# TensorE transposes in two halves with strided weight reads, and two weight preparations moved earlier

## The chip, the cores and the metric

The kernel runs on one NeuronCore of a Trainium2 chip. The metric is device time of one execution in microseconds (us), lower is better; the median of several runs is compared. The engines are TensorE (PE, matrix products; its weight loads are listed apart as PEld), VectorE (DVE), ScalarE (ACT), GpSimd (POOL) and SyncE (SP). SP, ACT and POOL issue DMA transfers. Each engine works through its own instructions in order and waits on semaphores for the others.

## The reference

All arrays are fp32: x is (4, 512, 512), so there are four batches b of 512 rows. The first half is a gated scan, the second a feed-forward network (FFN) with a Hadamard transform:

```python
n = layernorm(x)
i, f, g = n @ Wi.T, n @ Wf.T, n @ Wg.T
gate = sigmoid(f);  v = silu(i) * (1 - gate)
o[t] = gate[t] * o[t-1] + v[t]                  # along the 512 rows of a batch
o = o * rsqrt(mean(o*o) + eps) * gnorm_w * silu(g)
x = x + layernorm(o @ Wo.T)
h = layernorm(x)
h = fwht(silu(h @ W1.T) * (h @ W3.T))           # 2048 wide, scaled by 1/sqrt(2048)
x = x + layernorm(h @ W2.T)
```

The Hadamard transform stands between h and W2, so the kernel applies it to W2 once instead of to every h.

## The kernel before, in words

**Seven products.** Every matrix product is done with Strassen's scheme in Winograd's form: both operands are split in 2x2 blocks, sums of blocks are formed ("combined") by DVE, and seven block products P1, P2, P6, P5, P7, P3, P4 are issued in this order by `seven` (line 378). The left operand has the sums S1 to S4 (`combine_left`, lines 120 to 125), the right one T1 to T4 (`combine_right`, lines 127 to 132). P1 and P2 use plain blocks. P6 is the first that needs sums, S2 and T2. The products go to three PSUM banks X, Y and Z: P1, P6, P7 and P4 to X, P2 to Y, P5 and P3 to Z. ACT copies P1, P6, P5 and P4's new values out of the bank and DVE adds the others (lines 400 and 402), and a product that adds to a bank has to wait until the bank's values of the step before are read.

**Units.** `attn_unit(b, u)` computes the projections of one batch: u = 0 and 1 are Wi and Wf for two halves of the columns, followed by the gates and the scan; u = 2 is Wg, followed by the output gate and the normalisation's squares. `attn_out(b)` multiplies by Wo, adds to x, and normalises the result for the FFN. `ffn_unit(b, m)`, m = 0 to 7, computes W1 and W3 for a share of the 2048 columns, and `ffn_out(b, part)` multiplies two units' results by W2.

**Order on PE.** PE and SP run in exactly the order in which the program is written. A queue `fill` holds small steps of other work; `run` (line 97) takes one step from it after each of the seven products where the unit is dense, or after the second, fourth, sixth and seventh where it isn't. The order on DVE, ACT and POOL is chosen by a scheduler from priorities (`tc.high_priority`) and from `behind(what)` (line 207), which holds instructions back until the instruction recorded as `read[what]` has been placed.

**Activations on PE's right side.** `normalize_tiles` (line 236) computes mean and variance of 128 rows by DVE (lines 251, 252), the power by POOL (line 221), the bias by DVE (line 229), and applies them with one ACT instruction a tile (line 262). Three batches' inputs (`ON_TENSOR`, line 234: the scan's input of batches 0 and 1 and the FFN's of batch 0) are then transposed by PE in `transpose` (line 323): 16 transposes of 128x128 (line 334) into four PSUM banks, copies by ACT and DVE (lines 339 and 341), and the sums T1 to T4. For these the ACT instruction reads its row permuted, every fourth element first, so that the columns of each transpose lie side by side. The other batches go through DRAM and a 32x32 DVE transpose.

**Weights.** Wi, Wf, Wg, W1 and W3 are loaded with batch 0 or 1, combined by DVE (`combine_weights`), stored to DRAM in combined form by POOL (`kept`, line 138), and loaded again for the next batches (`again`, line 145). Wo is scaled by gnorm_w, combined and stored by `prepare_wo` (line 585). W2 is transformed in two steps: the high step multiplies eight pieces (`load_w2`, line 614; `transform_high`, line 624) by a 128x128 Hadamard matrix and stores them; the low step reads eight tiles back (`load_low`, line 635), multiplies them by a block-diagonal one (`transform_low`, line 653), combines and stores them. High steps fill the units of batch 0, low steps the FFN units of batch 0. Weight tiles lie in two pools, five buffers and four; a load into a buffer waits until the last reader of its old content is done, and all loads behind it in SP's queue wait with it.

Of the kernel before, what the change touches and what calls it, by code (L numbers as in the profile page):

```python
# [11 lines left out]
F32 = mybir.dt.float32  # L12
AF = mybir.ActivationFunctionType
ALU = mybir.AluOpType
P = 128
# [27 lines left out]
def kernel(  # L43
# [41 lines left out]
    def bank(name):  # L85
        return psum.tile([P, 2, H], F32, tag="ps", name=name)
# [146 lines left out]

    ON_TENSOR = ("a", 0), ("a", 1), ("f", 0)

    def normalize_tiles(b, name, i0, n):

        if (name, b) not in xns:
            xns[name, b] = work.tile(
                [P, NT, D], F32, tag="wide", name=f"xn_{name}_{b}", bufs=3
            )
        t = xns[name, b]
        st = small.tile([P, n, 6], F32, tag=f"st{n}", name=f"st_{name}_{b}_{i0}")
        mv = small.tile([P, n, 2], F32, tag=f"mv{n}", name=f"mv_{name}_{b}_{i0}")
        for k in range(n):  # L250
            nc.vector.bn_stats(st[:, k, :], xs[b][:, i0 + k, :])
            nc.vector.bn_aggr(mv[:, k, :], st[:, k, :])
        r, nb, read["nb"] = scales(mv, EPS, f"{name}_{b}_{i0}")
        for k in range(n):
            x_t, to = xs[b][:, i0 + k, :], t[:, i0 + k, :]
            if (name, b) in ON_TENSOR:
                x_t = x_t.rearrange("p (k c) -> p c k", c=ND)
                to = to.rearrange("p (c k) -> p c k", c=ND)
            else:
                x_t = x_t.rearrange("p (i a c) -> p i c a", c=ND, a=32)  # L260
                to = to.rearrange("p (i c a) -> p i c a", c=ND, a=32)
            nc.scalar.activation(  # L262
                to, x_t, AF.Identity, bias=nb[:, k : k + 1], scale=r[:, k : k + 1]
            )
        if (name, b) not in ON_TENSOR:
            if (name, b) not in xnd:
                xnd[name, b] = scratch.tile(
                    [NT, P, D], F32, tag=f"xn_{name}_{b}", name=f"xnd_{name}_{b}"
                )
            nc.gpsimd.dma_start(  # L270
                out=xnd[name, b][i0 : i0 + n].rearrange("t p d -> p t d"),
                in_=t[:, i0 : i0 + n, :],
            )

    def normalize(b, name, n=2):
        for i in range(0, NT, n):
            normalize_tiles(b, name, i, n)
# [42 lines left out]

    xts = {}

    def transpose(b, name):

        xn = xns.pop((name, b))
        xt = work.tile([P, 7, 2, H], F32, tag="xt", name=f"xt_{name}_{b}", bufs=2)
        pt = [bank(f"pt_{name}_{b}_{c}") for c in range(ND)]  # L330
        for h in range(2):
            for i in range(2 * h, 2 * h + 2):
                for c in range(ND):
                    nc.tensor.transpose(pt[c][:, h, ts(i % 2, P)], xn[:, i, ts(c, P)], ident)
        with tc.high_priority(offset=URGENT):
            for c in range(ND):
                to = xt[:, B11 : B12 + 1 : B12 - B11] if c < 2 else xt[:, B21 : B22 + 1]
                if c % 2:
                    nc.scalar.copy(to[:, :, c % 2, :], pt[c])
                else:  # L340
                    nc.vector.tensor_copy(to[:, :, c % 2, :], pt[c])  # L341
            combine_right(xt, nc.vector)
        xts[name, b] = xt

    folds = {}

# [29 lines left out]
    def seven(name, multiply, quarter, done=None, add=False, by_tile=False):  # L376

        ps = {}

        def make(what, a, bb, which, first):
            if first:
                ps[which] = bank(f"{which}_{name}")
            multiply(ps[which], a, bb, first)
            split = by_tile and what == "P4"  # L390
            q = {"P1": (0, 0), "P5": (1, 1), "P6": (0, 1), "P2": (0, 0), "P7": (1, 1),
                 "P3": (0, 1), "P4": (1, 0)}[what]
            to = quarter(*q)
            with tc.high_priority(offset=URGENT):
                if split:
                    for t in range(2):
                        nc.vector.tensor_add(to[:, t], ps[which][:, t], to[:, t])
                        done(*q, t)
                elif what in ("P2", "P7", "P3") or add:
                    read[what] = nc.vector.tensor_add(to, ps[which], to)  # L400
                else:
                    nc.scalar.copy(to, ps[which])  # L402
# [36 lines left out]
    def attn_unit(b, u, dense=False):  # L439
        def gates(d):  # L440

            v, gate = d[:, 0], d[:, 1]
            nc.scalar.activation(gate, gate, AF.Tanh, scale=0.5)
            nc.scalar.activation(v, v, AF.Silu)
            nc.vector.scalar_tensor_tensor(v, gate, 1.0, v, ALU.subtract, ALU.mult)
            nc.scalar.activation(gate, gate, AF.Identity, bias=half_t, scale=0.5)
            if u == 0:
                os_[b] = work.tile([P, 2, 2, T], F32, tag="o", name=f"o_{b}")
            for h in range(2):
                nc.vector.tensor_tensor_scan(  # L450
                    os_[b][:, u, h, :], gate[:, h, :], v[:, h, :], 0.0, ALU.mult, ALU.add
                )

        def output_gate(d):
            o = os_[b]
            og = work.tile([P, 7, 2, H], F32, tag="og", name=f"og_{b}")
            nc.scalar.activation(d, d, AF.Silu)
            for m in range(2):
                into_left(og, o[:, m], d[:, m], m)
            combine_left(og, nc.vector)  # L460
            ogs[b] = og
            nc.scalar.activation(o, o, AF.Square)
            nc.vector.tensor_add(o[:, 0], o[:, 0], o[:, 1])
            nc.vector.tensor_add(o[:, 0, 0], o[:, 0, 0], o[:, 0, 1])
# [117 lines left out]
        )  # L582


    def prepare_wo():
        w = [stream_tile(("wo", c), 0, stream2) for c in range(2)]
        for c in range(2):
            for k, blocks in enumerate(((B11, B12), (B21, B22))):
                row = (2 * k + c) * P
                nc.sync.dma_start(  # L590
                    out=w[c][:, blocks[0] : blocks[1] + 1 : blocks[1] - blocks[0]],
                    in_=wo[row : row + P].rearrange("p (n f) -> p n f", n=2),
                )
            for k, blocks in enumerate(((B11, B12), (B21, B22))):
# [5 lines left out]
        wo_t[0] = w  # L600

    NR = FF // P
    NJ = NR // 2
# [60 lines left out]

    load_w2(range(0, 1))
    load_x(0)
    load_w2(range(1, 2))
    load_attn_w(0, 0)
    load_w2(range(2, 4))
    load_attn_w(0, 1)  # L670
    load_w2(range(4, 6))
    load_x(1)
# [1 line left out]
    load_attn_w(0, 2)  # L674
    with tc.high_priority():
        normalize(0, "a", 1)
    with behind("power"):
        for make in high(0, 2):
            make()
    transpose(0, "a")  # L680
    with behind("nb"):
        combine_weights(2)
    with behind("power"):
        load_constants()
    fill.extend(high(2, NJ))
    attn_unit(0, 0)
    with behind("P2"):
        combine_weights(2)
    attn_unit(0, 1, True)
    with behind("P2"):  # L690
        normalize(1, "a")
    with behind("P3"):
        combine_weights(2)
    load_attn_w(1, 0)
    attn_unit(0, 2)
    with behind("P3"):
        prepare_wo()
    transpose(1, "a")
    while len(fill) > 1:
        slot()  # L700
    fill.extend([None] * 3 + attn_out(0))
    attn_unit(1, 0, True)
    load_attn_w(1, 1)
    attn_unit(1, 1, True)
    load_attn_w(1, 2)
    load_ffn_w(0, 0)
    load_low(0)
    load_low(1)
    attn_unit(1, 2)
    transpose(0, "f")  # L710
    combine_weights()
    for b in range(B):
        last = b == B - 1
        for m in range(NU):
            if m + 1 < NU:
                load_ffn_w(b, m + 1)
            if b == 0 and m % NS == 0:
                for k in range(m, m + NS):
                    fill.extend(transform_low(k))
            if m == 0 and not last:  # L720
                fill.extend([None] * 4 * (b > 0) + attn_out(b + 1))
# [12 lines left out]
            if m == NU - 1 and not last:  # L734
                transpose_fold(*((b + 2, "a") if b + 2 < B else (b + 1, "f")))
            ffn_unit(b, m, b == 0)
            combine_weights()
        tail = ffn_out(b, NU // NS - 1)
        if b + 2 < B:
            load_attn_w(b + 2, 0)  # L740
# [52 lines left out]
```

## Time and profile before

| | |
|---|---|
| median of 3 runs | 849.2 us (847.85 to 849.77) |
| profiled execution | 848.68 us |
| its span, first to last instruction | 846.9 us |
| PE busy | 817.6 us, 97% |
| DVE, ACT, POOL busy | 459.0, 274.3, 69.4 us |
| DMA | 169.54 MB, mean 200 GB/s |
| granted PE clock | 0.996 |

The program takes its first 46 us with the DMA engines almost fully busy, its last 10 us without PE, and PE is nearly always busy in between. Times in the text are microseconds from the start of the span, where nothing else is said. "X waits for Y" means that the engine stood idle before X until Y ended, as the profiler's semaphore events show. A matmul of fp32 values appears as two records, a transpose as one.

### The profile page before, as it was taken

To read this page: it belongs to the slowest core of one execution; us is meant where nothing else is said; L and a number is where in the kernel's file an instruction comes from. 1 tells how busy PE (TensorE), PEld (TensorE's weight loads), DVE (VectorE), ACT (ScalarE), POOL (GpSimd) and SP (SyncE) were. 2 spreads that over 40 slices of the span, in tenths; PEclk is the share of its full clock that TensorE was granted. 3 is DMA by queue.
4 is the path that set the end of the run, shared out by engine and by line. 5 is a ranking of instruction groups with operands and counts; after the bars stand their busy time and mean duration, and the time that the engine had idled before them with its cause. 6 is when DMAs were issued, how large, how long until landed. Compare 5 with 4: busy or idle time off the path is not lost.

```text
span 846.9 us, 9792 instructions
## 1 busy us (share of the span) xinstructions
PE 817.6 (97%) x3728; PEld 701.1 (83%) x3728; DVE 459.0 (54%) x914; ACT 274.3 (32%) x376; POOL 69.4 (8%) x112
## 2 busy tenths in 40 slices
PE   5999989999999999999999999999999999999995
PEld 3778868878878888888888888888888888888884
DVE  5458667674747556548245544836335434633445
ACT  4563364352412224425421122424322121222111
POOL 4110010120201001002100000101100000100000
PEclk9999999999999999999999999999999999999998
DMA  9976376668889823925563822754343742625101
GB/s 331 399 260 274 113 238 235 243 257 318 300 290 346 245 87 110 405 106 199 170 231 116 266 87 87 283 202 175 136 179 94 299 158 103 224 87 217 62 26 50
DMA packets 65743, 169.54 MB, mean 200 GB/s; under 512 B 4768, under 2 KB 40224, under 8 KB 65696
## 3 DMA queue, kind: packets, MB, share of 16 engines
q1 hardware_dynamic: 56528, 125.65, 42.5%
q0 software_dynamic: 8448, 41.96, 12.4%
q10 hardware_dynamic: 720, 1.31, 0.4%
q8 instruction: 29, 0.48, 0.2%
q14 instruction: 18, 0.15, 0.0%
HBM read 125.90 MB, written 42.99 MB: 199 GB/s over the span
## 4 chain that ended last, share of the span: by engine, by line
PE 81%; DVE 6%; DMA 4%; ACT 4%; issue 2%; POOL 1%; SPq 0%; POOLq 0%; ACTq 0%; DVEq 0%
PE X_f L415 23%; PE X_po L548 11%; PE Z_f L415 11%; PE X_a L415 8%; PE Z_po L548 6%; PE Y_f L415 5%; PE Z_a L415 4%; PE X_y L501 3%; PE Y_po L548 3%; PE Y_a L415 2%; PE Z_y L501 2%; ACT xn_a L262 1%; DMA wi<-s_wi 1%; DMA x<-in_x_dram 1%; PE Y_y L501 1%
## 5 line engine op out<-in xcount | busy, mean ns | idle before, releaser
L415 PE MATMUL X_f<-xt_f,w 128*128 128x256 f32 x1024 | 242.2, 380 | 2.0 <-ACT d_f L402 1.1
L415 PEld LDWEIGHTS X_f<-xt_f,w 128*128 128x128 f32 x1024 | 193.7, 190 | 33.9 <-ACT d_f L402 3.3
L402 ACT COPY d_f<-X_f 128x512 f32<-128x512 f32 x96 | 56.1, 584 | 302.6 <-PE X_f L415 278.3
L415 PE MATMUL Z_f<-xt_f,w 128*128 128x256 f32 x512 | 121.2, 379 | 0.4 <-ACT d_f L402 0.4
L548 PE MATMUL X_po<-w,ht 128*128 128x256 f32 x512 | 120.9, 379 | 0.2 <-DVE f L400 0.2
L415 PEld LDWEIGHTS Z_f<-xt_f,w 128*128 128x128 f32 x512 | 97.1, 190 | 16.0 <-ACT d_f L402 1.2
L548 PEld LDWEIGHTS X_po<-w,ht 128*128 128x128 f32 x512 | 97.2, 190 | 13.7 <-DVE f L400 0.6
L400 DVE TENSOR_TENSOR f<-X_po,f 128x512 f32<-128x512 f32 x51 | 35.1, 689 | 90.4 <-PE X_po L548 90.1
L430 DVE TENSOR_TENSOR ht<-d_f 128x1024 f32<-128x1024 f32 x32 | 39.0, 1219 | 66.7 <-ACT d_f L524 53.0
L548 PE MATMUL Z_po<-w,ht 128*128 128x256 f32 x256 | 60.6, 379 | 1.8 <-DVE f L400 1.8
L415 PE MATMUL Y_f<-xt_f,w 128*128 128x256 f32 x256 | 60.5, 379 | 0.0
L548 PEld LDWEIGHTS Z_po<-w,ht 128*128 128x128 f32 x256 | 48.6, 190 | 8.7 <-DVE f L400 2.2
L415 PEld LDWEIGHTS Y_f<-xt_f,w 128*128 128x128 f32 x256 | 48.6, 190 | 8.3 <-issue 1.2
L221 POOL TENSOR_TENSOR rs_f<-rs_f,power 128x2 f32<-128x2 f32 x16 | 15.8, 990 | 442.4 <-DVE nm_f L304 419.6
L402 ACT COPY d_a<-X_a 128x512 f32<-128x512 f32 x36 | 21.1, 586 | 90.8 <-PE X_a L415 74.6
L400 DVE TENSOR_TENSOR d_f<-X_f,d_f 128x512 f32<-128x512 f32 x32 | 22.1, 690 | 27.0 <-PE X_f L415 27.0
L400 DVE TENSOR_TENSOR d_f<-Z_f,d_f 128x512 f32<-128x512 f32 x32 | 22.1, 689 | 26.4 <-PE Z_f L415 26.4
L415 PE MATMUL X_a<-xt_a,wi 128*128 128x256 f32 x128 | 33.1, 381 | 1.3 <-DVE xt_a L341 1.3
L524 ACT ACTIVATE d_f<-d_f 128x1024 f32<-128x1024 f32 x32 | 33.8, 1055 | 0.9
L415 PE MATMUL X_a<-xt_a,wg 128*128 128x256 f32 x128 | 30.4, 381 | 2.5 <-ACT d_a L402 1.6
L415 PE MATMUL X_a<-xt_a,wf 128*128 128x256 f32 x128 | 32.8, 379 | 0.0
L415 PEld LDWEIGHTS X_a<-xt_a,wi 128*128 128x128 f32 x128 | 24.1, 190 | 8.1 <-issue 3.3
(154 smaller groups left out, 998.8 us busy)
## 6 DMA issues: line engine op xcount, KB each, us to landing
w<-s_w SPq DMA_DIRECT2D x80, 896.0 KB, 6.3
s_w<-w POOLq DMA_DIRECT2D x24, 896.0 KB, 5.0
w<-in_W_dram SPq DMA_DIRECT2D x32, 256.0 KB, 5.9
wi<-s_wi SPq DMA_DIRECT2D x6, 896.0 KB, 10.3
wf<-s_wf SPq DMA_DIRECT2D x6, 896.0 KB, 7.4
wg<-s_wg SPq DMA_DIRECT2D x6, 896.0 KB, 5.2
wo<-s_wo SPq DMA_DIRECT2D x6, 896.0 KB, 9.4
w_h<-w2p POOLq DMA_DIRECT2D x8, 512.0 KB, 7.2
```

Source lines behind the costliest of these rows:

```text
L221: read["power"] = nc.gpsimd.tensor_tensor(r, r, power_t[:, 0:n], ALU.pow)
L262: nc.scalar.activation(to, x_t, AF.Identity, bias=nb[:, k : k + 1], scale=r[:, k : k + 1])
L400: read[what] = nc.vector.tensor_add(to, ps[which], to)
L402: nc.scalar.copy(to, ps[which])
L415: nc.tensor.matmul(ps[:, n, :], w[:, a, c, :], xt[:, bb, c, :], start=first and n == 0 and c == 0, stop=c == 1, skip_group_check=True,)
L430: nc.vector.tensor_mul(to.rearrange("p (t k) f -> p k t f", t=2), a.rearrange("p k (t f) -> p k t f", t=2), b2.rearrange("p k (t f) -> p k ...
L501: nc.tensor.matmul(ps[:, t, :], og[:, a, c, ts(t, P)], w[c][:, bb, :], start=first and t == 0 and c == 0, stop=c == 1, skip_group_check=True,)
L524: nc.scalar.activation(d[:, 0], d[:, 0], AF.Silu)
L548: nc.tensor.matmul(ps[:, t, :], hts[b, m][:, a, ts(t, P)], w[m][:, bb, :], start=first and t == 0 and m == ms[0], stop=m == ms[-1], skip_g ...
```

## The change

1. The ACT instruction of the three batches on PE reads and writes its rows in order. Instead the transpose reads its operand, which PE loads as weights, with a step of four elements (`xn[:, i, c::ND]`).
2. `transpose` becomes `transposes`, which returns two steps, one for each half of the rows. Each step does eight transposes and its own copies; the right sums follow the second. The steps are put into `fill`, so that they run between the products of the unit before (for batch 0: the first half in front, the second after the first product).
3. In batch 0 the third piece of w2 is loaded ahead of wi and wf; ACT's copies for the second and third piece are held behind the normalisation; unit 0 is dense and unit 1 isn't.
4. Batch 1's normalisation moves from unit 1 to unit 2, its statistics behind P3 of unit 1 and its ACT instructions behind a copy in unit 2.
5. Wo is loaded ahead of batch 1's wi and wf, and prepared behind P2 of unit 2.
6. The low steps 0 and 1 of w2 run in batch 1's units 1 and 2, and those of the FFN units run two tiles further on. Their loads move with them in SP's queue.
7. The Silu of the output gate is done in two halves, and weights are combined behind P7 of the unit before.

```diff
-        for k in range(n):
-            x_t, to = xs[b][:, i0 + k, :], t[:, i0 + k, :]
-            if (name, b) in ON_TENSOR:
-                x_t = x_t.rearrange("p (k c) -> p c k", c=ND)
-                to = to.rearrange("p (c k) -> p c k", c=ND)
-            else:
...
+        def apply():
+            for k in range(n):
+                x_t, to = xs[b][:, i0 + k, :], t[:, i0 + k, :]
+                if (name, b) not in ON_TENSOR:
...
+                read["xn"] = nc.scalar.activation(
+                    to, x_t, AF.Identity, bias=nb[:, k : k + 1], scale=r[:, k : k + 1]
...
+        if later:
+            return apply
+        apply()
...
-    def transpose(b, name):
+    def transposes(b, name):
...
+        def make(h):
+            if h == 0:
+                pt.extend(bank(f"pt_{name}_{b}_{c}") for c in range(ND))
             for i in range(2 * h, 2 * h + 2):
                 for c in range(ND):
-                    nc.tensor.transpose(pt[c][:, h, ts(i % 2, P)], xn[:, i, ts(c, P)], ident)
...
+                    nc.tensor.transpose(pt[c][:, h, ts(i % 2, P)], xn[:, i, c::ND], ident)
+            with tc.high_priority(offset=URGENT):
+                for c in range(ND):
+                    to = xt[:, (B11, B12)[h] if c < 2 else (B21, B22)[h], c % 2, :]
+                    if c % 2:
+                        nc.scalar.copy(to, pt[c][:, h, :])
+                    else:
+                        read["xt"] = nc.vector.tensor_copy(to, pt[c][:, h, :])
+                if h:
+                    combine_right(xt, nc.vector)
+        return [partial(make, h) for h in range(2)]
...
-            nc.scalar.activation(d, d, AF.Silu)
             for m in range(2):
+                nc.scalar.activation(d[:, m], d[:, m], AF.Silu)
                 into_left(og, o[:, m], d[:, m], m)
...
-    load_w2(range(1, 2))
+    load_w2(range(1, 3))
     load_attn_w(0, 0)
-    load_w2(range(2, 4))
+    load_w2(range(3, 4))
...
+    first, second = transposes(0, "a")
     with behind("power"):
-        for make in high(0, 2):
+        for make in high(0, 1):
             make()
-    transpose(0, "a")
-    with behind("nb"):
+        with behind("xn"):
+            for make in high(1, 2) + [first] + high(2, 3):
+                make()
+    with behind("xt"):
         combine_weights(2)
...
-    fill.extend(high(2, NJ))
-    attn_unit(0, 0)
+    fill.extend([second] + high(3, NJ))
+    attn_unit(0, 0, True)
     with behind("P2"):
         combine_weights(2)
-    attn_unit(0, 1, True)
-    with behind("P2"):
-        normalize(1, "a")
+    attn_unit(0, 1)
     with behind("P3"):
-        combine_weights(2)
+        with tc.high_priority(offset=URGENT):
+            combine_weights(2)
+        with tc.high_priority(offset=SOON):
+            apply = [normalize_tiles(1, "a", i, 2, True) for i in (0, 2)]
+    wo_t[0] = load_wo()
     load_attn_w(1, 0)
...
+    fill.extend([wo_behind_sum, norm_behind_copy] + transposes(1, "a"))
     attn_unit(0, 2)
-    with behind("P3"):
-        prepare_wo()
-    transpose(1, "a")
-    while len(fill) > 1:
-        slot()
+    load_attn_w(1, 1)
     fill.extend([None] * 3 + attn_out(0))
     attn_unit(1, 0, True)
-    load_attn_w(1, 1)
-    attn_unit(1, 1, True)
-    load_attn_w(1, 2)
-    load_ffn_w(0, 0)
     load_low(0)
     load_low(1)
+    load_attn_w(1, 2)
+    fill.extend(transform_low(0) + transform_low(1))
+    attn_unit(1, 1, True)
+    load_ffn_w(0, 0)
+    fill.extend(transposes(0, "f"))
     attn_unit(1, 2)
-    transpose(0, "f")
-    combine_weights()
+    with behind("P7"):
+        combine_weights()
...
-                for k in range(m, m + NS):
+                for k in range(m + 2, min(m + 2 + NS, NU)):
                     fill.extend(transform_low(k))
...
             ffn_unit(b, m, b == 0)
-            combine_weights()
+            with behind("P7"):
+                combine_weights()
```

`prepare_wo` is split into `load_wo`, which issues the four loads and returns the tiles, and `prepare_wo(w)`, which does the rest; `wo_behind_sum` calls it behind P2, and `norm_behind_copy` calls the two held `apply` steps behind an ACT copy.

More of the change, by code (lines that the diff above doesn't have):

```diff
@@ L234, with normalize_tiles @@
     ON_TENSOR = ("a", 0), ("a", 1), ("f", 0)
-    def normalize_tiles(b, name, i0, n):
+    def normalize_tiles(b, name, i0, n, later=False):
         if (name, b) not in xns:
@@ L253, in normalize_tiles @@
         r, nb, read["nb"] = scales(mv, EPS, f"{name}_{b}_{i0}")
-        for k in range(n):
-            x_t, to = xs[b][:, i0 + k, :], t[:, i0 + k, :]
-            if (name, b) in ON_TENSOR:
-                x_t = x_t.rearrange("p (k c) -> p c k", c=ND)
-                to = to.rearrange("p (c k) -> p c k", c=ND)
-            else:
[L260 to L268, printed above, removed]
-                )
[L270 to L273, printed above, removed]
+        def apply():
+            for k in range(n):
+                x_t, to = xs[b][:, i0 + k, :], t[:, i0 + k, :]
+                if (name, b) not in ON_TENSOR:
+                    x_t = x_t.rearrange("p (i a c) -> p i c a", c=ND, a=32)
+                    to = to.rearrange("p (i c a) -> p i c a", c=ND, a=32)
+                read["xn"] = nc.scalar.activation(
+                    to, x_t, AF.Identity, bias=nb[:, k : k + 1], scale=r[:, k : k + 1]
+                )
+            if (name, b) not in ON_TENSOR:
+                if (name, b) not in xnd:
+                    xnd[name, b] = scratch.tile(
+                        [NT, P, D], F32, tag=f"xn_{name}_{b}", name=f"xnd_{name}_{b}"
+                    )
+                nc.gpsimd.dma_start(
+                    out=xnd[name, b][i0 : i0 + n].rearrange("t p d -> p t d"),
+                    in_=t[:, i0 : i0 + n, :],
+                )
+        if later:
+            return apply
+        apply()
     def normalize(b, name, n=2):
@@ L321 @@
     xts = {}
-    def transpose(b, name):
+    def transposes(b, name):
         xn = xns.pop((name, b))
         xt = work.tile([P, 7, 2, H], F32, tag="xt", name=f"xt_{name}_{b}", bufs=2)
-        pt = [bank(f"pt_{name}_{b}_{c}") for c in range(ND)]
-        for h in range(2):
+        xts[name, b] = xt
+        pt = []
+        def make(h):
+            if h == 0:
+                pt.extend(bank(f"pt_{name}_{b}_{c}") for c in range(ND))
             for i in range(2 * h, 2 * h + 2):
                 for c in range(ND):
[L334 to L343, printed above, removed]
+                    nc.tensor.transpose(pt[c][:, h, ts(i % 2, P)], xn[:, i, c::ND], ident)
[9 more added lines that the diff above has]
+        return [partial(make, h) for h in range(2)]
     folds = {}
@@ L401, in make @@
                 else:
-                    nc.scalar.copy(to, ps[which])
+                    read["copy"] = nc.scalar.copy(to, ps[which])
             if what in ("P2", "P7", "P3", "P4") and done is not None and not split:
@@ L582, in ffn_out, with load_wo @@
         )
-    def prepare_wo():
+    def load_wo():
         w = [stream_tile(("wo", c), 0, stream2) for c in range(2)]
@@ L593, in prepare_wo @@
                 )
+        return w
+    def prepare_wo(w):
+        for c in range(2):
             for k, blocks in enumerate(((B11, B12), (B21, B22))):
@@ L599, in prepare_wo @@
             kept(("wo", c), w[c])
-        wo_t[0] = w
     NR = FF // P
@@ L684, with wo_behind_sum, norm_behind_copy @@
         load_constants()
-    fill.extend(high(2, NJ))
-    attn_unit(0, 0)
+    fill.extend([second] + high(3, NJ))
+    attn_unit(0, 0, True)
     with behind("P2"):
         combine_weights(2)
-    attn_unit(0, 1, True)
-    with behind("P2"):
-        normalize(1, "a")
+    attn_unit(0, 1)
     with behind("P3"):
-        combine_weights(2)
-    load_attn_w(1, 0)
-    attn_unit(0, 2)
-    with behind("P3"):
-        prepare_wo()
-    transpose(1, "a")
-    while len(fill) > 1:
-        slot()
+        with tc.high_priority(offset=URGENT):
[3 more added lines that the diff above has]
+    wo_t[0] = load_wo()
+    load_attn_w(1, 0)
+    while fill:
+        slot()
+    def wo_behind_sum():
+        with behind("P2"):
+            prepare_wo(wo_t[0])
+    def norm_behind_copy():
+        with behind("copy"):
+            for make in apply:
+                make()
+    fill.extend([wo_behind_sum, norm_behind_copy] + transposes(1, "a"))
+    attn_unit(0, 2)
+    load_attn_w(1, 1)
     fill.extend([None] * 3 + attn_out(0))
     attn_unit(1, 0, True)
-    load_attn_w(1, 1)
-    attn_unit(1, 1, True)
-    load_attn_w(1, 2)
-    load_ffn_w(0, 0)
     load_low(0)
     load_low(1)
+    load_attn_w(1, 2)
[3 more added lines that the diff above has]
+    fill.extend(transposes(0, "f"))
     attn_unit(1, 2)
-    transpose(0, "f")
-    combine_weights()
+    with behind("P7"):
+        combine_weights()
     for b in range(B):
```

## The prediction

> **What bounds it now.** I read the table of engines first, then the chain that ended last, then what TensorE (PE) waited for, then the windows and the timeline of the first 125 us.
>
> ```profile
> PE 817.6 (97%) x3728; PEld 701.1 (83%) x3728; DVE 459.0 (54%) x914; ACT 274.3 (32%) x376; POOL 69.4 (8%) x112
> PE 81%; DVE 6%; DMA 4%; ACT 4%; issue 2%; POOL 1%; SPq 0%; POOLq 0%; ACTq 0%; DVEq 0%
> ```
>
> PE is busy for 817.6 of 846.9 us. The change keeps all of PE's matmuls, so it can win only from the 29.3 us in which PE stands idle, and lose by new idle time or by making a PE instruction longer. The windows (columns: stretch, its length, then busy us of PE first) say where the idle time is:
>
> ```profile
> 0.00:18.05 18.05, 8.38 (x24) 3.80 (x24) 7.72 (x29) 9.08 (x11) 7.56 (x19) 1.00 0.89 314
> 18.05:46.00 27.95, 27.95 (x113) 21.58 (x114) 14.78 (x30) 12.08 (x18) 5.84 (x11) 1.00 1.02 394
> 46.00:68.90 22.90, 20.89 (x96) 16.55 (x94) 13.60 (x29) 15.59 (x20) 3.95 (x7) 1.00 0.76 284
> 68.90:110.00 41.10, 40.96 (x192) 35.69 (x192) 29.17 (x61) 17.49 (x26) 3.16 (x5) 1.00 0.44 165
> 110.00:125.00 15.00, 11.41 (x57) 9.39 (x58) 10.91 (x23) 9.48 (x10) 2.64 (x3) 1.00 0.68 238
> 410.00:830.00 420.00, 419.56 (x1945) 368.57 (x1945) 197.60 (x351) 103.58 (x149) 13.35 (x19) 1.00 0.44 156
> ```
>
> Idle: 9.7 us before 18.05, 2.0 to 68.9, 3.6 in 110 to 125, 3.5 to 410, 10.0 after 830. The last 10 us are an epilogue that the change leaves alone. The list of PE's waits names the rest:
>
> ```profile
> PE h L624 <- DMA w2p<-in_W_dram: 5.7, 1, 5.7
> PE pt_a L334 <- ACT xn_a L262: 3.5, 4, 1.9
> PE Z_a L415 <- ACT d_a L402: 1.9, 2, 1.2
> PE Z_po L548 <- DVE f L400: 1.8, 1, 1.8
> PE X_a L415 <- ACT d_a L402: 1.6, 1, 1.6
> ```
>
> The first 5.7 us are the first load. The transposes of batch 0 then wait 3.5 us for ScalarE's (ACT's) normalisation. Its duration and that of the same form without a permuted read, then the transposes' weight loads and matmuls (min/median/max ns):
>
> ```profile
> L262 ACT ACTIVATE xn_a<-x,nb_a,rs_a 128x512 f32<-128x512 f32 x16 | 20.4, 1320 | 5.2 <-DVE nb_a L229 5.2
> L307 ACT ACTIVATE y<-y,nm_y 128x512 f32<-128x512 f32 x16 | 10.6, 712 | 3.9 <-DVE nm_y L304 3.9
> L334 PEld LDWEIGHTS pt_a<-ident,xn_a x32: 138/140/143, 13.3 to 67.7; 128*128 128x128 f32 x32
> L334 PE MATMUL pt_a<-ident,xn_a x32: 272/273/329, 13.3 to 67.8; 128*128 128x128 f32 x32
> 66.21 1.91 PE L334 MATMUL pt_a<-ident,xn_a 128*128 128x128 f32 x16
> ```
>
> Sixteen transposes in 1.9 us: 0.117 us each.
>
> [...]
>
> **The parts, and their cost.** A product below is 1.73 us of PE (eight records 0.216 apart), a 128x512 transform of w2 is 0.86, a 128x256 VectorE (DVE) pass advances its queue by 0.34, a 128x512 one by 0.6, a 128x1024 one by 1.2.
>
> *The stride.* 48 transposes, three batches of 16, now load weights from every fourth column. Nothing in the trace shows this. Below: 0, if the load stays under its matmul. Nearest row: ACT's read rate halves, [...] and the pace 0.22, +0.10 us each, 4.9 us for 48. [...] I take 0.22: eight transposes then take 1.76 us, not 0.93.
>
> *Start of batch 0.* Before, ACT copied four transform results, the last at 11.48 to 12.07, before its first normalisation at 11.96. Now two come first; the second ended at 10.07, and the bias was ready at 9.95. At 0.72 a tile, overlapping, the first two tiles are ready at 11.45 and all at 12.7 (16.88 before). PE finishes the second w2 piece at 11.45, and then runs: eight transposes to 13.2, two transforms of the third piece to 14.9, first product to 16.7, eight transposes to 18.4, second product to 20.1, one transform to 21.0. Before, the third product (P6) began at 22.47 with two fewer transforms done. Gain 22.47 - 21.0 + 1.72 = 3.2. The third piece is loaded ahead of wi and wf on SP's queue: 0.5 MB at about 0.4 MB/us makes wf land near 13.4, not 12.1, hidden behind 14.9. DVE's chain (two copies, eight combinations, two copies, two xt sums) has S2 and T2 near 20.6, just before P6. The fifth w2 piece, needed near 25.3, landed at 27.1 before; with stores starting later I put it near 25 and charge 0, with 1.8 as the other end.
>
> *Unit 1 and 2 of batch 0.* The normalisation of batch 1 leaves unit 1: its 1.23 us wait (PE at 47.99 for an ACT copy behind a 1.29 us normalisation) goes. Fewer fillers add 0.25, where P6 waits for a copy behind ACT's tanh, table load and silu. Gain 1.0. Unit 2 before ran 53.27 to the next unit's P6 at 72.60: 19.33, less one transform, 18.47, with the 0.83 wait at 68.95 in it. After: six products to 10.35, transposes to 12.1, the last product at 12.55 (DVE's add of P7 sits behind combinations of wg, statistics, two scans and seven wo passes, some 15 us in one queue), to 14.3; the second half waits for DVE's copies of the first, which stand behind three wo passes and an add, to 16.5; two products to 19.95. P6 needs T2, behind two copies, two output-gate multiplies and T1: 21.1. Queued behind it are all other PE products. Loss 2.7. The split Silu lets the first multiply start 1 us sooner; it is in this sum. wo, now ahead of batch 1's wi and wf on SP, takes the slot of stored w2 pieces and is wanted 8 us after it can land; wi and wf are wanted 14 us after their slots are free.
>
> *Batch 1 to the FFN.* From P5's end in unit 1 (99.39) to the FFN's first product (124.78) were 25.39 us, with waits of 1.63, 0.69, 0.90 and 0.65. ACT's order is the cause: four normalisations of 1.32 between copies. Now they take 0.72, and four moved transforms (3.45 us) give cover. I find one wait left, 0.45. New length 25.39 - 3.87 + 0.45 + 3.45, and 1.66 for the stride: gain 3.42 - 1.66 = 1.8 after taking off work that is only moved. The FFN's first two products need the first half alone; T2 is done 4 us before its P6. Pulling low tiles 2 and 3 forward makes SP wait for the wo slots (last product of batch 0's output, about 101) ahead of the FFN's first weights, which still land 8 us before use. Their eight DVE sums and POOL stores run where DVE is busy 0.7 and POOL 0.08.
>
> *FFN of batch 0.* The 1.78 us wait at 240.51 is DVE behind a weight load; that load stood on SP behind w2 tiles waiting for a store at 222 to 231. Those tiles are now fetched two units earlier, and the combinations come behind P7: 1.5 gained. Were the store the limit elsewhere, 1.8 would come back. Combining behind P7 leaves 11 us to the next P6 for 2.7 us of DVE.
>
> *At nothing.* The copies out of PSUM become twice as many of half the size: 2 x 0.34 against 0.6 of DVE's queue each, 0.5 us for six, inside the chains above. Later batches are transposed by DMA and DVE as before; from 410 on no instruction changes, and PE idles 0.4 us there.
>
> Sum: 3.2 + 1.0 - 2.7 + 1.8 + 1.5 = 4.8. The profiled execution took 848.68 (span 846.9 and 1.8 around it); the median is 0.5 above it. Forecast 849.2 - 4.8 = 844.4.
>
> **Rivals.** *Stride free.* For it: the transposes' weight load is 140 ns, the others' 190, so it may have room under its matmul. Then 4.9 less about 1.7 that DVE and DMA waits take: +3.2, time 841.2.
> *Strided loads decide against it.* Place: the 48 transposes on PE. Without stride the gain is 8.0; some 85% of added time lies on the path, so 48 x 0.85 x e = 8.0 at e = 0.20, a pace of 0.31. [...] Against it: ACT pays only a factor of two.
> *New waits take the start's gain.* The DMA engines are 0.89 to 1.02 busy until 46; if the fifth piece lands at 27.1 or wg late, and DVE's queue in unit 2 runs 2 us longer than my sum, the 3.2 to 3.8 won go: 848.
>
> **Chances.** Forecast 0.42, free stride 0.25, waits 0.15, dear stride 0.18. Under 0.2% (1.7 us) no difference can be told in this kernel. Faster: 0.42 + 0.25 + 0.07 = 0.74; same 0.08, half of the waits case; slower 0.18. The forecast's own range, with its DMA and DVE ends, is 841 to 848. The full range, 838.5 to 851, reaches past the free stride (with no DVE waits left) and leaves out most of the dear stride, 0.14, and 0.05 below.
>
> **What would show it.** The strided weight load near 245 ns and 16 transposes spread over some 3.5 us; the third product at 21 us; no normalisation wait of PE over 1 us; waits for DVE before the last product of unit 2 and the third of the next; no wait of 1.6 us near 111, none of 1.8 near 240. It is wrong if a transpose's pace passes 0.31, or if PE waits for a w2 piece before 40 us for over 3 us.

## The result and the profile after

The changed kernel takes 840.97 us (median of 4 runs, 840.72 to 841.86), the kernel before 849.45 (4 runs, 847.85 to 849.77). The ratio is 0.9906, 95% interval 0.9889 to 0.9923. The forecast was 844.4 with 838.5 to 851 around it. The profiled execution took 841.11 us with a span of 839.3, which is 7.57 us less than the execution before. The forecast gain was 4.8, and it comes near only because its errors have both signs.

The page of the changed kernel: engines, then the chain that ended last.

```profile
PE 817.5 (97%) x3728; PEld 703.8 (84%) x3728; DVE 457.6 (55%) x920; ACT 269.1 (32%) x386; POOL 68.9 (8%) x112
...
PE 84%; DVE 5%; DMA 5%; ACT 2%; issue 2%; SPq 1%; POOL 1%; POOLq 0%; DVEq 0%; ACTq 0%
```

PE is busy for as long as before (817.5 and 817.6 us), so the gain is idle time. DMA and SP's queue, 4% and 0% of the chain before, are 5% and 1% now. The windows (stretch, length, then busy us of PE first) and the list of PE's waits (total, times, longest):

```profile
0.00:18.05 18.05, 13.04 (x45) 7.84 (x46) 9.68 (x33) 9.08 (x16) 8.07 (x20) 1.00 0.94 325
...
46.00:68.90 22.90, 22.06 (x107) 18.76 (x106) 22.02 (x49) 15.45 (x22) 5.37 (x7) 1.00 1.02 399
...
110.00:125.00 15.00, 15.00 (x73) 12.51 (x72) 14.63 (x28) 8.23 (x14) 1.06 (x2) 1.00 0.60 213
```

```profile
PE h L638 <- DMA w2p<-in_W_dram: 5.2, 2, 5.0
PE Z_f L426 <- ACT d_f L413: 4.7, 2, 4.5
...
PE X_a L426 <- DVE xt_a L130: 0.8, 1, 0.8
```

Up to 125 us, PE has lost all its waits but three: the first load, 0.18 us for a w2 piece at 35.45 and 0.84 us for T2 at 66.25. But there is a wait that the forecast doesn't have: 4.5 us for a copy by ACT, in unit 4 of batch 0's FFN. By stages, from the starts of the same products in both timelines (work that is only moved taken out):

| stage | forecast gain | measured | how |
|---|---|---|---|
| start to batch 0's third product | 3.2 | 5.4 | 22.47 to 18.74, and two transforms more done; 0.7 of it is the first load, 5.70 to 5.01 |
| units 1 and 2, to the next third product | -1.7 | 0.9 | 72.60 to 66.25, less the 5.4 above |
| batch 1 to the FFN's first product | 1.8 | 4.35 | 124.78 to 117.53, less the time won so far, and 3.45 of transforms done |
| FFN of batch 0 | 1.5 | -3.3 | 409.81 to 402.40 at a later wait that both have, less all the above |
| rest | 0 | 0.2 | |
| sum | 4.8 | 7.6 | |

So two readings had to be tested: that the strided read costs PE next to nothing, and that the FFN's new wait is made by x of batch 2 coming late, and by which part of the change.

The transposes and the normalisation up to 70 us, by tile (min/median/max ns):

```profile
L343 PEld LDWEIGHTS pt_a<-ident,xn_a x32: 195/209/221, 10.3 to 61.6; 128*128 128x128 f32 x32
```

```profile
L262 ACT ACTIVATE xn_a<-x,nb_a,rs_a x8: 799/802/815, 9.4 to 57.3; 128x512 f32<-128x512 f32 x8
```

The weight load went from 140 to 209 ns, but eight transposes started at 57.96 and the product behind them at 58.91: 0.119 us each from start to start, where the forecast has 0.117 for contiguous columns. ACT's tile went from 1320 to 802 ns.

The chain that ended last, in the changed kernel near the new wait (start, us, what):

```profile
195.91 12.70 DMA x<-in_x_dram
...
208.63 0.69 DVE st_a L252
...
213.18 1.28 ACT xn_a L262
214.46 0.48 ACT d_f L413
...
214.98 3.78 PE Z_f L426 x8
```

x of batch 2 takes 12.7 us from issue to landing. DVE's statistics wait for it, POOL's power and ACT's normalisation follow, and the copy that PE needs is queued behind the second normalised tile. Which transfers stand beside x's? First the timeline of the kernel before, then that of the changed one (start, us, queue, line, what):

```profile
199.96 0.53 POOL L138 DMA_DIRECT2D s_w<-w  x1 [1.63 <-DVE w L125]
...
204.18 2.11 SPq L116 DMA_DIRECT2D x<-in_x_dram  x4
```

```profile
195.44 2.22 SPq L116 DMA_DIRECT2D x<-in_x_dram  x4
...
196.03 0.53 POOL L138 DMA_DIRECT2D s_w<-w  x1 [19.21 <-DVE w L125]
```

The two stores of combined weights, 896 KB each, were issued at 197.80 and 199.96 before, 6.4 and 4.2 us ahead of x. Combining behind P7 put them at 196.03 and 197.03, 0.6 and 1.6 us behind x's first issue. The DMA engines, 0.05 busy from 188 to 194 us, are 1.00 and 1.04 busy in 198 to 204 and 204 to 210. (Both kernels also issue two 896 KB reloads of down weights just ahead of x.) x's median landing went from 8.0 to 12.6 us. An estimate: two stores are 1.8 MB, which take 4.6 us at the 400 GB/s of 204 to 210 us, as much as x lost.

The wait costs more than its length. The windows around it (the third number from the end is PE's granted clock):

```profile
210.00:215.00 5.00, 0.53 (x4) 0.12 (x2) 2.61 (x13) 3.02 (x4) 2.43 (x4) 0.84 0.84 251
215.00:217.50 2.50, 2.50 (x6) 2.05 (x7) 0.65 (x1) 2.50 (x3) 0.48 (x1) 0.50 0.95 388
217.50:220.00 2.50, 2.50 (x7) 1.96 (x7) 2.17 (x6) 0.30 (x1) 1.25 (x2) 0.50 0.90 372
```

After the idle stretch of 4.47 us PE runs at half clock (0.50) for 5 us, from 215 to 220, and at 0.95 from 220 to 222. The product that waited takes 3.58 to the next one's start and that one 2.54, in place of 1.73 each: 4.47 + 1.85 + 0.81 = 7.1 us.

### The profile page after: what moved, and what is told of

Its sections match the earlier page's. It is cut to its first block, busy times and chain, and to the rows that moved or that the text cites. A ratio compares the mean times of both kernels' runs of the same rounds, so it can differ in the third digit from the quotient of the medians.

```text
span 839.3 us, 9824 instructions
## 1 busy us (share of the span) xinstructions
PE 817.5 (97%) x3728; PEld 703.8 (84%) x3728; DVE 457.6 (55%) x920; ACT 269.1 (32%) x386; POOL 68.9 (8%) x112
## 3 DMA queue, kind: packets, MB, share of 16 engines
q0 software_dynamic: 8448, 41.96, 12.7%
## 4 chain that ended last, share of the span: by engine, by line
PE 84%; DVE 5%; DMA 5%; ACT 2%; issue 2%; SPq 1%; POOL 1%; POOLq 0%; DVEq 0%; ACTq 0%
PE X_f L426 23%; PE X_po L559 12%; PE Z_f L426 12%; PE X_a L426 8%; PE Z_po L559 6%; PE Y_f L426 6%; PE Z_a L426 5%; PE Y_po L559 3%; PE X_y L512 3%; DMA w2p<-in_W_dram 3%; PE Y_a L426 2%; PE Z_y L512 2%; DMA x<-in_x_dram 2%; DVE x L316 1%; PE Y_y L512 1%
## 5 line engine op out<-in xcount | busy, mean ns | idle before, releaser
L426 PE MATMUL Z_f<-xt_f,w 128*128 128x256 f32 x512 | 122.9, 384 | 4.7 <-ACT d_f L413 4.7
L221 POOL TENSOR_TENSOR rs_f<-rs_f,power 128x2 f32<-128x2 f32 x16 | 14.0, 878 | 428.7 <-DVE nm_f L308 406.8
L411 DVE TENSOR_TENSOR f<-Z_po,f 128x512 f32<-128x512 f32 x28 | 19.2, 684 | 24.9 <-PE Z_po L559 24.9
```

The source lines that it names most:

```text
L221: read["power"] = nc.gpsimd.tensor_tensor(r, r, power_t[:, 0:n], ALU.pow)
L426: nc.tensor.matmul(ps[:, n, :], w[:, a, c, :], xt[:, bb, c, :], start=first and n == 0 and c == 0, stop=c == 1, skip_group_check=True,)
```

## The experiments

The kernel before was timed again beside each group of runs. Its median was 849.67 to 849.84 us there and 849.45 beside the changed kernel, so the differences from the changed kernel below are uncertain by some 0.4 us on top of the ranges given.

### The strided weight load by itself

The kernel before, with six groups of 16 transposes put ahead of batch 1's own, differing only in the step of the columns. Their results are overwritten.

```diff
+        flat = xn.rearrange("p n d -> p (n d)")
+        if (name, b) == ("a", 1):
+            for k in range(16):
+                nc.tensor.transpose(pt[k % 4][:, k // 8, ts(k // 4 % 2, P)], flat[:, 0 : 128 : 1], ident)
+            for k in range(16):
+                nc.tensor.transpose(pt[k % 4][:, k // 8, ts(k // 4 % 2, P)], flat[:, 0 : 255 : 2], ident)
...
```

> The kernel before, with 96 more transposes put ahead of the real ones of batch 1 (six groups of 16, whose weights are 128 columns at every 1st, 2nd, 3rd, 4th, 8th and 16th fp32). Their results are overwritten, so the output is the same and the time is longer by some 12 us or more. Theory A (the slower weight load stays under the matmul before it): the weight load is near 140 ns at step 1 and 210 at step 4, [...]and rises no further at 8 and 16; steps 2 and 3 lie between; 16 transposes take 1.9 us at every step. Theory B [...]: 16 take 1.9 us at step 1 and 3.5 at step 4. A third way: the load rises again at 8 and 16 by what the bytes span[...].

It took 859.05 us in one run, beside 849.84 for the kernel before: 9.2 more, where 12 or more were expected. The tile's weight loads (lines 334, 336 and 340 are the steps 1, 2 and 4; 338, 342 and 344, left out, are 3, 8 and 16 with medians of 196, 192 and 196 ns), then PE's timeline:

```profile
L334 PEld LDWEIGHTS pt_a<-ident,xn_a x16: 139/141/142, 67.4 to 69.1; 128*128 128x128 f32 x16
L336 PEld LDWEIGHTS pt_a<-ident,xn_a x16: 194/209/209, 69.2 to 71.0; 128*128 128x128 f32 x16
...
L340 PEld LDWEIGHTS pt_a<-ident,xn_a x16: 206/211/213, 73.0 to 74.8; 128*128 128x128 f32 x16
```

```profile
67.61 1.91 PE L334 MATMUL pt_a<-ident,xn_a 128*128 128x128 f32 x16
69.35 2.08 PE L336 MATMUL pt_a<-ident,xn_a 128*128 128x128 f32 x16
...
73.08 2.10 PE L340 MATMUL pt_a<-ident,xn_a 128*128 128x128 f32 x16
75.02 1.94 PE L342 MATMUL pt_a<-ident,xn_a 128*128 128x128 f32 x16
```

Theory A holds for the pace and B falls: from one group's start to the next it is 1.74 us at step 1 and 1.94 at step 4, 0.0125 us more for a transpose, 0.6 us for 48. What theory A says of the steps between falls: step 2 loads as slowly as step 4 (209 and 211), and steps 3, 8 and 16 a little faster. Of the six steps only the contiguous one stands apart. And sixteen loads of 0.211 are 3.4 us, but lie within 2.0: the loads overlap each other, so their duration isn't their pace.

### The stride undone, and the stride alone

The first takes the strided read out of the changed kernel, the second puts only it into the kernel before.

```diff
-                if (name, b) not in ON_TENSOR:
+                if (name, b) in ON_TENSOR:
+                    x_t = x_t.rearrange("p (k c) -> p c k", c=ND)
+                    to = to.rearrange("p (c k) -> p c k", c=ND)
+                else:
...
-                    nc.tensor.transpose(pt[c][:, h, ts(i % 2, P)], xn[:, i, c::ND], ident)
+                    nc.tensor.transpose(pt[c][:, h, ts(i % 2, P)], xn[:, i, ts(c, P)], ident)
```

> The changed kernel with only the stride undone: ScalarE reads every fourth column again and the transposes read contiguous ones; order and halves stay as changed. Theory A (strided weight loads cost nothing on TensorE, ScalarE's shorter normalisation is the gain): a normalised tile takes 1.32 instead of 0.72 us, so TensorE waits for tiles 1 to 3 of batch 0 near 12 to 17 us; 2 to 4 us slower than the changed kernel, 843 to 845. Theory B (0.10 us for each of 48 strided transposes): it gains 4.9 us on TensorE and loses the same 2 to 4; 0 to 3 us faster than the changed kernel. If the wait near 215 us depends on ScalarE's timing early on, it could shift by a microsecond either way.

843.64 us (843.04 to 844.31), 2.7 slower than the changed kernel, as theory A has it. PE waits 1.07 at 15.60 and 0.88 at 109.80 for ACT, which it doesn't with the stride. The 4.48 us wait in the FFN stays.

```diff
-            if (name, b) in ON_TENSOR:
-                x_t = x_t.rearrange("p (k c) -> p c k", c=ND)
-                to = to.rearrange("p (c k) -> p c k", c=ND)
-            else:
+            if (name, b) not in ON_TENSOR:
...
-                    nc.tensor.transpose(pt[c][:, h, ts(i % 2, P)], xn[:, i, ts(c, P)], ident)
+                    nc.tensor.transpose(pt[c][:, h, ts(i % 2, P)], xn[:, i, c::ND], ident)
```

> The kernel before with only the stride: the transposes read every fourth column, ScalarE's normalisation of the transposed batches reads and writes without permutation. Theory A (the strided weight load is hidden, the normalisation takes 0.72 instead of 1.32): the waits for ScalarE at 13 to 17 us shrink from 3.5 to about 1.5, that at 48 us and those at 111 to 121 us by 1 to 3 together; 844 to 847. Theory B (0.10 us for each of 48 transposes on TensorE's path): 4.9 us of this are lost again, 848 to 852.

844.84 us (844.2 to 845.31) beside 849.74: ratio 0.9945, interval 0.9929 to 0.9961, in theory A's range. This small part alone gives 4.9 us, as much as the forecast charged for its strided reads; in the new order, by the run above, the same edit is worth 2.7. On PE's timeline the transposes now wait once:

```profile
12.36 2.86 PE L331 MATMUL pt_a<-ident,xn_a 128*128 128x128 f32 x16 [1.39 <-ACT xn_a L259]
```

The transposes' 3.5 us of waits are 1.39, all 16 go in one row, and the product behind them waits 0.42; the 1.63 at 111 us is 0.63, and the 0.69 for ACT near 118 is gone; the FFN's 1.7 us wait for DVE is as before.

### The start in its old order

The changed kernel with four transforms ahead of all 16 transposes, and the third w2 piece behind wi and wf.

```diff
-    load_w2(range(1, 3))
+    load_w2(range(1, 2))
     load_attn_w(0, 0)
-    load_w2(range(3, 4))
+    load_w2(range(2, 4))
...
-        for make in high(0, 1):
+        for make in high(0, 2):
             make()
-        with behind("xn"):
-            for make in high(1, 2) + [first] + high(2, 3):
-                make()
+    first()
+    second()
...
-    fill.extend([second] + high(3, NJ))
+    fill.extend(high(2, NJ))
```

> The changed kernel with the start of batch 0 in the old order: four transforms of w2 before the 16 transposes, these in one go, the third w2 piece behind wi and wf again. The strided read and the short normalisation stay. Theory A (the start gained 4.8 us by both, and the stride alone is 1.9 of it by the run with the permuted read): TensorE idles 2 to 4 us more before 20 us, the rest is as in the changed kernel, 843 to 845. Rival (the short normalisation alone is enough, since the tiles then come at 0.72 us each): less than 1 us slower, under 842.

843.57 us (842.39 to 844.3), 2.6 slower than the changed kernel. On PE's timeline the transposes wait 1.39 us at 12.05 for ACT's normalisation, and 0.25 and 0.21 behind that: 1.85 us of new idle time, a little under the 2 to 4 of theory A. The profiled spans differ by 1.3 only, so the size is uncertain. That the order adds to the short normalisation is clear: all four runs lie above the rival's 842.

### x one unit earlier

```diff
+            if m == 2 and b == 0:
+                load_x(2)
...
-            if m == 3 and b == 0:
-                load_x(2)
```

> The changed kernel, and the load of x of batch 2 is issued one FFN unit earlier (in unit 2 instead of unit 3 of batch 0), ahead of the w2 tiles and the down weights of that unit; its third buffer is free by then. Theory A (TensorE's 4.47 us wait at 215 us comes from x, which is issued at 195.4 and lands after 12.7 us, because VectorE and ScalarE do the statistics and the normalisation in order ahead of the unit's copies): the wait goes, with the slow clock behind it; 5 to 7 us faster than the changed kernel, 834 to 836. Rival (the DMA engines are full there, and whatever is moved only changes what is late): the down weights or w2 tiles come late instead, gain below 2 us, with a new wait for a DMA between 180 and 245 us.

834.36 us (834.05 to 834.73), ratio to the kernel before 0.9818, interval 0.9797 to 0.9839. This is 6.6 below the changed kernel, whose own ratio is 0.9906, and the fastest of all. From the list of PE's waits, the one in question:

```profile
PE Z_f L426 <- ACT d_f L413: 0.2, 1, 0.2
```

The 4.47 is gone, no other wait took its place, and the span is 7.0 shorter (832.3), against the 7.1 worked out above. Theory A holds: x's lateness was the whole of it. In 211 to 222 us PE was busy 7.02 of 11 us at clock 0.69 before this edit, and 11.00 of 11 at 1.00 with it.

### Which part makes x late

Two candidates: the order behind P7, which moved the stores, and w2's lower tiles, fetched two units earlier. The first is tried alone in the kernel before, the second undone in the changed one.

```diff
             ffn_unit(b, m, b == 0)
-            combine_weights()
+            with behind("P7"):
+                combine_weights()
```

> The kernel before with one edit: in the FFN loop the combinations of the next weights come behind the adds of P7. Theory A (this order takes a late weight load out of VectorE's way, and on the other side brings the stores beside the load of x): the 1.78 us wait at 240.5 goes; x of batch 2 lands later than its 8 us; if it is late enough, a wait for ScalarE's copy of 1 to 5 us comes near 219, so the time is between 847 and 853. Rival (the wait at 215 us of the changed kernel comes from the w2 tiles that are fetched two units earlier, not from this order): no wait over 1 us near 219, and the time is some 1.5 us below the kernel before.

855.14 us (853.72 to 855.54), ratio 1.0064, interval 1.0047 to 1.0082: slower than the kernel before, and 2 us past the range of theory A. PE waits 5.66 us at 225.10 for ACT's copy; in the timeline x and a store beside it, then DVE's statistics, stand ahead in that chain:

```profile
204.37 2.17 SPq L116 DMA_DIRECT2D x<-in_x_dram  x4
204.96 0.53 POOL L138 DMA_DIRECT2D s_w<-w  x1 [19.21 <-DVE w L125]
...
216.49 0.69 DVE L251 BATCH_NORM_STATS2 st_a<-x 128x6 f32<-128x512 f32 x1 [3.75 <-DMA x<-in_x_dram]
...
225.10 3.65 PE L415 MATMUL Z_f<-xt_f,w 128*128 128x256 f32 x8 [5.66 <-ACT d_f L402]
```

This one edit makes the wait, with no tile fetched earlier. x's median landing is 13.8 us. SP issues the down weights and x within 0.2 us of where it did in the kernel before (203.52 and 204.37, 203.32 and 204.18 before); of the transfers ahead of x and just behind it only the stores have moved, from 197.80 and 199.96 to 204.96 and 205.97. So it is the stores that make x late. The 1.78 us at 240.5 is gone, as the theory says.

```diff
+    attn_unit(1, 1, True)
+    load_attn_w(1, 2)
+    load_ffn_w(0, 0)
     load_low(0)
     load_low(1)
-    load_attn_w(1, 2)
-    fill.extend(transform_low(0) + transform_low(1))
-    attn_unit(1, 1, True)
-    load_ffn_w(0, 0)
...
-                for k in range(m + 2, min(m + 2 + NS, NU)):
+                for k in range(m, m + NS):
```

> The changed kernel without the lower transforms of w2 pulled forward: tiles 0 and 1 are loaded and transformed in the FFN again, and each pair in the unit where it was. Theory A (the four moved transforms cover ScalarE's copies at the end of batch 1): one or two waits of 0.5 to 1.6 us come back between 95 and 125 us, and a wait for VectorE behind a late weight load of 1 to 2 us near 235; the 4.47 us wait stays if the order behind P7 makes it, and goes if the early tiles do. With the wait staying 843 to 845; with it gone 836 to 838.

844.32 us (843.66 to 847.05), with this in PE's timeline:

```profile
216.25 3.78 PE L426 MATMUL Z_f<-xt_f,w 128*128 128x256 f32 x8 [5.88 <-ACT d_f L413]
```

The wait stays and is longer (x's median landing is 14.0), so the early tiles don't make it. The moved transforms cover one wait, 0.92 for DVE at 115.54; the wait of 1 to 2 us expected near 235 didn't come, so it is the order behind P7 that keeps it away, not the early tiles. A DMA wait of 1.63 at 37.6, where the changed kernel has 0.18, lies ahead of everything edited.

### Is the order behind P7 worth anything?

The changed kernel without it, with x late and with x early. Both drop the same line in the FFN loop:

```diff
-            with behind("P7"):
-                combine_weights()
+            combine_weights()
```

> The changed kernel without the order that puts the combination of the next FFN weights behind the adds of P7; the combinations' stores to memory come earlier again. Theory A1 (x of batch 2 lands late because stores of unit 4's weights were moved next to its load): the 4.47 us wait shrinks to below 1.5 us and the time is 4 to 6 us below the changed kernel, 835 to 837. Theory A2 (x is late because of the w2 tiles and down weights in front of it): x still takes over 11 us to land, the wait stays above 3 us, the time is within 1.5 us of the changed kernel.

843.87 us (843.64 to 844.38), 2.9 slower than the changed kernel. As A1 has it, the stores are early again (191.05 and 193.17), x lands after 7.8 us and the wait for ACT is 0.95. But A1's time is wrong: a new wait appears in the timeline.

```profile
231.68 0.42 DVE L122 TENSOR_TENSOR w<-w 128x256 f32<-128x256 f32 x1 [9.08 <-DMA w<-in_W_dram]
...
234.10 3.78 PE L559 MATMUL X_po<-w,ht 128*128 128x256 f32 x8 [5.04 <-DVE f L411]
```

DVE stands 9.08 us at a combination whose weights haven't landed, and the adds that PE needs are behind it. By the chain that ended last these weights were issued at 217.87 and landed after 13.1 us, and POOL issued four stores of 896 KB from 217.82 on: again stores beside a load that an in-order queue waits for. In the kernel before, DVE waits in the same way for 5.67 us up to 238.30, and PE loses its 1.78 at 240.51 by it; there the weights were issued late, at 231.69, and landed within 6.0.

> The changed kernel with both edits: x of batch 2 loaded one unit earlier, and no order behind P7. Theory A (the order behind P7 is worth the 5.04 us wait for VectorE behind a late weight load near 234, which the run without it showed, and has nothing to do with x once x is early): no wait near 214, a wait of 3 to 5 us near 232, 838 to 842. Rival (that wait was itself a follow-up of x's load between the weights): it goes too, 834 to 835.

836.65 us (836.29 to 838.0), below theory A's 838 and above the rival's 835. From its timeline:

```profile
228.95 1.99 PE L559 MATMUL X_po<-w,ht 128*128 128x256 f32 x8 [1.07 <-DVE f L411]
```

Neither alone: most of the 5.04 was a follow-up of x's load, and 1.07 is left. With x late, POOL stood 2.21 us at the store of batch 2's normalised rows, just ahead of the four stores of 217.82. With x early it has issued two by 211 and three from 215.37 on, and the weights, issued at 216.68 and 217.26, are combined at 226.52. With x early, the order behind P7 is worth 2.3 us.

### The control: x early in the kernel before

The same move of `load_x(2)` as above, in the kernel before.

> The kernel before with only the load of x of batch 2 one FFN unit earlier. Theory A (x comes just in time in the kernel before, so that its lateness is made by the order behind P7): the 0.23 us wait at 219.5 goes at most, the 1.78 us wait at 240.5 may move by a microsecond; within 1.5 us of the kernel before. Rival (x's load costs the kernel before too, through the DMA engines or ScalarE's queue): 3 us or more faster.

```diff
+            if m == 2 and b == 0:
+                load_x(2)
             if b == 0 and m % NS == 0:
...
-            if m == 3 and b == 0:
-                load_x(2)
```

846.26 us (845.36 to 848.59) beside 849.74; ratio 0.9969, interval 0.9953 to 0.9985. The median gain is 3.5 us, which is the rival's and not theory A's; the interval, 1.3 to 4.0 us, leaves both possible. The 0.23 at 219.5 goes, as expected, and the 1.78 at 240.51 too: the weights behind it were issued at 228.55 instead of 231.69. Ahead of them in SP's queue are w2 tiles that wait for a store of POOL's, and POOL issued the last of its stores there from 221.72 on instead of 224.03, where it stood behind batch 2's normalised rows. So x's place cost the kernel before about 2.0 us of idle time, through POOL's stores and other weights, and the changed kernel 7, through ACT.

## Why the prediction was right and wrong

**The stride: wrong.** The step that failed is "the pace 0.22", the author's estimate, which no trace showed: the load was to slow down as ACT's read does (1320 ns against 712), and the pace with it. The load's rise was 1.5-fold, from 140 ns to 209. Above all the pace was read off the duration. Loads overlap each other, so the pace went from 0.109 us (1.74 for 16) to 0.121, and the 4.9 us charged for 48 transposes were 0.6. Nor does the load's time grow with the step: step 2, at 209 ns, is as slow as step 4, at 211. The rival *stride free* had the stride right, and its 841.2 is near the measured time, but by the same cancelling: it too has nothing of the FFN's new wait.

**Start: right in kind, 1.5 too small.** Of the 2.2 between 5.4 and 3.2, the stride is about 1.3 (eight transposes took 1.24 and 0.95 instead of twice 1.76), and the first load's run-to-run 0.7 is no gain of the change. The fifth w2 piece, a doubt of 1.8, made a wait of 0.18; it was 0.39 and 1.63 in two of the runs, with nothing edited ahead of it, so the doubt was fair. The third product was forecast at 21 and came at 18.74.

**Unit 1: right; unit 2: wrong.** 1.0 was forecast for unit 1, and 1.1 came. The 2.7 us loss in unit 2 was 0.2. DVE was as full as forecast (22.02 busy of 22.90), but its chain shorter: P7's add ended 11.05 us after the unit's start, not 12.55, and T2 18.5, not 21.1. The sums of queued passes were too large by 1.5 and 1.1. Of the two waits named, only that for T2 is there, 0.84. No run takes apart what else was moved here (wo's load, the normalisation, the split Silu), so their shares stay open.

**Batch 1 to the FFN: right in mechanism, too small.** No wait is left, where 0.45 was forecast, and the 1.66 for the stride wasn't paid; these are 2.1 of the 2.55 missed. By the runs it is the short normalisation rather than the moved transforms that does most: the stride alone leaves 0.63 of the 1.63 at 111 us, and the moved transforms save 0.92.

**FFN of batch 0: one half right, sign wrong.** The wait at 240.51 went. But "combining behind P7 leaves 11 us to the next P6 for 2.7 us of DVE" looked at DVE alone. Every combination also issues two stores of 896 KB, and the step didn't ask what is on the DMA engines at the new place. The sequence is: stores beside x, x 4.6 us later, statistics, normalisation, copy, PE. The run with that edit alone shows it. What is more, of a wait of over 4 us the forecast's accounting would have missed the half clock behind it (0.50 for 5 us after 4.47). With the 7.1 us of the new wait taken out the FFN gained 3.8, more than the 1.5: besides the 1.78, four waits of about 0.2 us are gone, which together are 2.6 of it.

**The sum.** The stages before the FFN gave 10.7 instead of 3.3, and the FFN took 3.3 instead of giving 1.5. The time lay within the full range, just under the 841 to 848 that the forecast calls its own, and in the likeliest direction, but the forecast's own working doesn't explain it. Without the FFN's wait it would have been near the 834.36 of the run with x early, below the whole range. That it lay inside is luck: costs that weren't there and a wait that wasn't seen cancelled in part.

## What to carry to other kernels

The duration of a pipelined instruction need not be its pace (here 16 weight loads of 0.211 us each lay within 2.0 us): take the pace from the start of one to the start of the next, and where only a duration is known to grow, keep "costs nothing" among the likely cases (0.0125 us for a transpose in this case). When an edit moves a computation, list the transfers that it issues, and look at which load stands beside them at the new place and who waits for that load in order. A load that several in-order queues hang on is worth trying as early as its buffer allows; here moving that one line gave 6.6 us, where the whole change gave 8.5.

## What the runs showed of the hardware that was not expected

- A 128-column fp32 weight load took 141 ns with contiguous columns and 192 to 211 ns (medians) with steps of 2, 3, 4, 8 and 16, but 16 transposes went from 1.74 to 1.94 us at most.
- ACT's 128x512 normalisation took 0.80 us with a contiguous read and 1.32 with a step of four.
- Waits of PE of 4.45 to 5.88 us in six kernels were each followed by a product of 3.42 to 3.78 us instead of 1.89, and the second behind it took up to 3.06. After waits of up to 1.78 us a product took 1.99. The long waits cost from 1.3 (5.66 us, where only one product was slow) to 1.6 times their length (4.47 us).
- A load of x, four transfers of 256 KB, landed after 7.8 to 8.0 us (medians) with two stores of 896 KB issued 4 to 8 us ahead of it, and after 12.6 to 14.0 with them issued 0.6 to 1.6 us behind its first transfer.
